# Strassen chains with two additions, a third PSUM bank seeded from the first, and x's first two tiles loaded and turned ahead of the others

## The chip, the cores and the metric

The kernel runs on one core of a Trainium2 chip. The metric is the device time of one execution in microseconds. Before the change it is 2528.57 us, the median of three runs (2528.29 to 2528.87).

In the profile's names PE is TensorE, DVE VectorE, ACT ScalarE, POOL GpSimd and SP SyncE. PEld is TensorE's weight load.

## The reference

Two graph-attention layers over a dense adjacency matrix, a residual and a layernorm, then one binary graph convolution with a residual and a layernorm. N is 3327 rows of 512.

```python
def _gat_layer(x, W, adj):
    proj = x @ W
    Wh, Ws = jnp.split(proj, 2, axis=-1)
    scores = Wh @ Ws.T
    a = jax.nn.softmax(scores, axis=-1) * adj
    out = a @ Wh
    out = out + x
    return jax.nn.leaky_relu(out, NEG_SLOPE)
...
x = _layernorm(x + gat(gat(x)))
bw = jnp.sign(weight)
ba = jnp.maximum(jnp.sign(x), 0.0)
x = _layernorm(x + relu(adj @ (ba @ bw.T)))
```

## The kernel before

Rows are cut into 26 tiles of 128. Two tiles are a pair or half (13 of them, `NQ`), four tiles a column chunk c (7 of them, `NC`; chunks 0 to 5 hold two halves, chunk 6 one). Everything on TensorE is f32, and one f32 product of 128x128 by 128x256 shows as two matmuls.

Each of the two layers has two stages. **Projection** (`project`, 0 to 185 us and 1229 to 1387 us): x's tiles are loaded and turned, the values `wh` are computed per pair, and the queries `g` per chunk. Both use Strassen's scheme with seven products (`seven`, L180): left sums S1 to S4, right sums T1 to T4, seven products over three PSUM banks Z, X and Y, and additions that join them into c11, c12, c21 and c22. The operands for the next stage are stored in HBM: keys per pair (`xs_d`: A11, A12, A21, A22, S1 to S4), values (`ws_d`) and queries per chunk (`gs_d`: B11, B21, B22, T1 to T4). Lists of steps are interleaved by `weave`. Layer 0 starts with x's first four tiles (`transpose_first`), whose turns, the first chain, and the turns of the weights (`transpose_w`, tile pwT, copied out to wTs) alternate.

**Attention** (`attention`, the rest): for every chunk c and pair q one score chain of seven products of two k-halves, spread over two steps (s = 0 and 1), and for every (g, q) one values step. Scores run `LOOK` = 30 steps ahead of the values, so the first 30 steps of a layer hold scores alone. A step's work is a list of (position, action), sorted by position; that is the program order of every engine. In a score chain: z1, x2, add11, z6 and y5 in the first step, z7, add22, y3, add12 and z4 in the second. A product's result that another addition needs is copied out of PSUM by ScalarE (p1, u2, p5, u3); add11 and add22 are VectorE additions, add11 and add12 with one PSUM operand, add22 (L648) with two SBUF operands. c21 is a ScalarE copy of Z.

After a half's last pair its column maximum is taken (`column_max`): fold and turn (L699, L702), a reduction (L703), four tiny copies that bring 32-row parts together (L709), a reduction (L710), three tiny copies (L714), and a transpose that spreads the result into the SBUF tile `off` (L719). A values step then subtracts `off` from a score tile (`shift`, L763), takes the exponential on ScalarE, multiplies with the adjacency, adds the running total, and feeds seven products (L839). When a half is finished its total is turned on TensorE in a PSUM tile of its own (`norm` in `finish`, L890).

SP issues all loads in program order, POOL's queue nearly all stores. Key tiles `xs` are loaded per chain in two parts (512 and 384 KB), each with two buffers, and the query tile `gs` (seven parts of 256 KB for a whole chunk, two buffers) in seven loads spread over the chunk before. `ws` has three buffers, `adj` four.

The finale multiplies the binary parts, and ends with the last three row tiles: a linear part (pxw), moments, root and `scaled`, which stores.

Before any of this, 20 small matmuls (`beat`) run on TensorE.

Of the kernel before, what the change touches and what calls it, by code (L numbers as in the profile page):

```python
# [9 lines left out]
F32 = mybir.dt.float32  # L10
# [19 lines left out]
DRUM = 20  # L30
# [3 lines left out]
def kernel(  # L34
# [44 lines left out]
    SBUFS = LOOK + 3  # L79
# [5 lines left out]
    with tc.manual_schedule():  # L85
        make_identity(nc, ident)
        drum = keep.tile([P, P], BF16, name="drum")
        nc.vector.memset(drum, 0.0)
        beat = ps_tr.tile([P, P], F32, tag="tr", name="beat")
        for n in range(DRUM):  # L90
            nc.tensor.matmul(beat, drum, drum, start=True, stop=True)
# [23 lines left out]
    xs_d = [tc.dram_tile([NQ, P, 8, 2, P], F32, name=f"xs_d{l}") for l in range(L)]  # L115
    ws_d = [tc.dram_tile([NQ, P, 4, HD], F32, name=f"ws_d{l}") for l in range(L)]
    gs_d = [
        [tc.dram_tile([P, 7, 2, len(halves_of(c)) * P], F32, name=f"gs_d{l}_{c}")
         for c in range(NC)] for l in range(L)
# [57 lines left out]
    S1, S2, A11, A12, A21, A22, S3, S4 = range(8)  # L177
    B11, B21, B22, T4, T1, T2, T3 = range(7)

    def seven(lane, name, multiply, c11, c12, c21, c22):  # L180
# [10 lines left out]
        def copied(i, b):  # L191
            if not held:
                two = slot([P, 2, HW], F32, f"h0_{name}"), slot([P, 2, HW], F32, f"h1_{name}")
                held.update(zip(("p1", "p5", "u2", "u3"), (t[:, e] for t in two for e in (0, 1))))
            nc.scalar.copy(held[i], bank[b])

        def add(to, a, b):
            nc.vector.tensor_tensor(to, a, b, ALU.add)

        return [  # L200
            lambda: (product(1, "Z", True), copied("p1", "Z")),
            lambda: (product(2, "X", True), add(c11, bank["X"], held["p1"])),
            lambda: (product(6, "Z", False), copied("u2", "Z")),
            lambda: (product(5, "Y", True), copied("p5", "Y")),
            lambda: (product(7, "Z", False), copied("u3", "Z"),
                     add(c22, held["p5"], held["u3"])),
            lambda: (product(3, "Y", False), add(c12, bank["Y"], held["u2"])),
            lambda: (product(4, "Z", False), nc.scalar.copy(c21, bank["Z"])),
# [27 lines left out]

    ch_lane, acc_lane, tr_lane = (ps_ch, "ch"), (ps_acc, "acc"), (ps_tr, "tr")
# [9 lines left out]
    def key_sums(l, q, a, xT, between=lambda: None):  # L247
# [6 lines left out]
            A22: xT[:, 2:4, j2], S1: s12[:, 0], S2: s12[:, 1], S3: s34[:, 0],  # L254
            S4: s34[:, 1], "s12": s12, "s34": s34,
# [4 lines left out]
        return of  # L260

# [37 lines left out]
    def sums_w(l):  # L299


        wsum_of[l] = ops.tile([P, 4, 2, HD], F32, tag="gs", name=f"wsum_{l}")
# [28 lines left out]
    def project(l, pre):  # L331
# [4 lines left out]
        def load_x(c):  # L336
            rows_of[c] = []
            for t in tiles_of(c):
# [11 lines left out]
        def transpose_first(lane):  # L350

            pool, tag = lane
            xTs[0] = pre.tile([P, KD, CW], F32, tag="xT", bufs=2, name=f"xT_{l}_0")
            pts = [pool.tile([P, CW], F32, tag=tag, name=f"pxt_{l}_{k}") for k in range(KD)]
            xts = [t.rearrange("r (p k) -> r k p", k=KD) for t in rows_of[0]]

            for a in range(CT):
                for k in range(KD):
                    nc.tensor.transpose(pts[k][:, ts(a, P)], xts[a][:, k], ident)
                if a % 2:  # L360
                    for k in range(KD):
                        half = ts(a // 2, HW)
                        copy_out(k, xTs[0][:, k, half], pts[k][:, half])
# [7 lines left out]
        if l == 0:  # L371
            load_x(0)
        else:
            xTs[0] = x_first[l]
        wa = pre.tile([P, KD, D], F32, tag="wa", bufs=1, name=f"wa_{l}")
        for k in range(KD):
            nc.sync.dma_start(out=wa[:, k], in_=w_rows_of(l, 0, k))
        if l == 0:
            load_w(l, 1)
            for k in range(KD):  # L380
                w_rows[l, 0, k] = wa[:, k]
        load_x(1)
        if l == 0:
            transpose_first(acc_lane)
# [17 lines left out]
        def keys(c, a, between=lambda: None):  # L402

            q = c * CT // 2 + a
            of = keys_first.pop((l, q), None) or key_sums(l, q, a, xTs[c], between)
            to = xs_d[l][q]
            for raw in (A11, A12, A21, A22):
                nc.gpsimd.dma_start(out=to[:, raw], in_=of[raw])
            nc.gpsimd.dma_start(out=to[:, S1 : S2 + 1], in_=of["s12"])
            nc.gpsimd.dma_start(out=to[:, S3 : S4 + 1], in_=of["s34"])  # L410
            return of

        def project_values(c, a, lane, between=lambda: None):
# [18 lines left out]

            return (
# [4 lines left out]
        def queries(c, lanes):  # L438
# [15 lines left out]
            if len(halves_of(c)) == 1:  # L454
# [14 lines left out]
                return None, [lambda e=e: one(e) for e in range(KD)] + [last_sums], []  # L469
# [29 lines left out]
            return sums, one, two + [done]  # L499
# [11 lines left out]
        chains, pairs_of, rest = {}, {}, []  # L511
# [6 lines left out]
        if l == 0:  # L518
# [6 lines left out]
            turns = [lambda k=k: transpose_w(l, 0, k, tr_lane) for k in range(KD)]  # L525
            turns += [second.pop(0), lambda: None]
            turns += [lambda k=k: transpose_w(l, 1, k, tr_lane) for k in range(KD)]
            for do in first + second[:2]:
                do()
                turns.pop(0)()  # L530
            second = second[2:]
# [10 lines left out]
        for c in range(NC):  # L542
            turns = []
            if c + 1 < NC:
# [3 lines left out]
                pairs_of[c + 1] = project_values(c + 1, 0, acc_lane)  # L548
                turns += [pairs_of[c + 1].pop(0), lambda: prepare(c + 1)]
            turns = rest + turns  # L550
            rest = [chains[c][1].pop()] if chains[c][1] else []
# [4 lines left out]
            else:  # L556
                one, two = chains[c]
                pairs = pairs_of[c]
                for a in range(1, len(tiles_of(c)) // 2):
                    pairs += project_values(c, a, acc_lane)  # L560
                rest.append(pairs.pop())
                weave(one + two, pairs, turns)
# [12 lines left out]
    def attention(l, att):  # L575
# [8 lines left out]

        def load_gs(c, i, n=1):
            if i == 0:
                gs[c] = ops.tile(
                    [P, 7, 2, len(halves_of(c)) * P], F32, tag="gs", bufs=2, name=f"gs_{l}_{c}"
                )
            nc.sync.dma_start(out=gs[c][:, i : i + n], in_=gs_d[l][c][:, i : i + n])  # L590

        def load_xs(c, q):
            for i, (a, n) in enumerate(((S1, 4), (A22, 3))):
                t = ops.tile([P, 4 - i, 2, P], F32, tag=f"xs{i}", name=f"xs{i}_{l}_{c}_{q}")
                nc.sync.dma_start(out=t[:, :n], in_=xs_d[l][q][:, a : a + n])
                for e in range(n):
                    xs[c, q, a + e] = t[:, e]

        def product(c, q, bank, a, b, start):
# [4 lines left out]
            for k in range(2):  # L604
                nc.tensor.matmul(  # L605
                    ch[bank], xs[c, q, a][:, k], gs[c][:, b, k],
                    start=(start and k == 0), stop=(k == 1), skip_group_check=True,
                )

        def scores(c, q, s):  # L610


# [12 lines left out]
            def z1():  # L625
                product(c, q, "Z", A11, B11, True)
                copied("p1", "Z")

            def x2():
                product(c, q, "X", A12, B21, True)  # L630

            def add11():
                nc.vector.tensor_tensor(c11, ch["X"], ch["p1"], ALU.add)

            def z6():
                product(c, q, "Z", S2, T2, False)
                copied("u2", "Z")
# [5 lines left out]
            def z7():  # L643
                product(c, q, "Z", S3, T3, False)
                copied("u3", "Z")

            def add22():
                nc.vector.tensor_tensor(c22, ch["p5"], ch["u3"], ALU.add)  # L648
# [6 lines left out]

            def z4():
# [3 lines left out]
            def maximum(i):  # L660
                t = sc[i, q]
                if q == NQ - 1 and pad:
                    nc.vector.tensor_scalar(
                        t[:, 1], t[:, 1], there[:, 0:1], there[:, 1:2], ALU.mult, ALU.add
                    )
                if q == 1:
# [742 lines left out]
```

## Time and profile before

| what | us |
|---|---|
| median of three runs | 2528.57 |
| the profiled execution, time | 2527.47 |
| its span | 2525.7 |
| TensorE busy | 2506.7 |
| VectorE busy | 2026.5 |
| POOL busy | 1463.2 |
| ScalarE busy | 783.6 |
| DMA, mean | 249 GB/s, 628.83 MB |

The span covers the work on the engines; the time of an execution has 1.8 us around it. A row of a group reads: line, engine, operation, output<-input, shape, number, then busy us in total, mean ns of one, and the idle time before it with what ended it. The granted TensorE clock was 0.999 of full over the span. Times of timeline rows are from the span's start.

### The profile page before, as it was taken

Reading aid. Unit: us, or ns where it says so; the run is one execution under the profiler, and the core shown is the slowest. Engines: PE = TensorE matmul, PEld = TensorE weight load, DVE = VectorE, ACT = ScalarE, POOL = GpSimd, SP = SyncE. Lnnn points to the kernel's source line nnn. Section 1 sums busy time; section 2 is a strip of 40 time slices with the busy share of each in tenths; the row PEclk is TensorE's granted clock in tenths of the full one; section 3 lists DMA queues with packets and bytes.
Section 4 is the critical chain, followed back from the end, with each engine's and each line's share of the span. In section 5 each row is a group of like instructions: output and inputs, shape, how many; then the busy total and the mean of one; then the engine's idle time right before and its main releaser. Section 6 shows DMA issues by size and latency. Waiting matters only on the chain.

```text
span 2525.7 us, 39290 instructions
## 1 busy us (share of the span) xinstructions
PE 2506.7 (99%) x12257; PEld 2185.0 (87%) x12257; DVE 2026.5 (80%) x3755; ACT 783.6 (31%) x1823; POOL 1463.2 (58%) x2302
## 2 busy tenths in 40 slices
PE   9999999999999999999999999999999999999998
PEld 7888888888888888898888888888888888899876
DVE  5765878789787897869876587888888888898977
ACT  3323333333333233222232333332333323322234
POOL 2652566766666666556655256566666666655631
PEclk9999999999999999999999999999999999999999
DMA  6858777777767767797885877777777777778984
GB/s 207 295 199 236 231 248 231 248 251 238 247 232 250 250 230 241 251 320 264 261 290 206 252 238 241 249 251 259 238 255 244 248 258 236 245 261 302 311 283 165
DMA packets 311394, 628.83 MB, mean 249 GB/s; under 512 B 35819, under 2 KB 166755, under 8 KB 310924
## 3 DMA queue, kind: packets, MB, share of 16 engines
q1 hardware_dynamic: 278254, 529.13, 64.3%
q0 software_dynamic: 32896, 97.09, 10.4%
q8 instruction: 100, 1.64, 0.3%
q14 instruction: 114, 0.93, 0.1%
q10 hardware_dynamic: 30, 0.03, 0.0%
HBM read 528.54 MB, written 97.58 MB: 248 GB/s over the span
## 4 chain that ended last, share of the span: by engine, by line
PE 94%; DVE 4%; issue 1%; POOL 1%; DMA 0%; ACT 0%; SPq 0%; ACTq 0%; DVEq 0%; POOLq 0%
PE acc L839 37%; PE pZ L605 22%; PE pY L605 11%; PE pX L605 6%; PE pZ_wh L421 4%; PE pZ_g L483 3%; PE agg L1137 3%; PE pY_wh L421 2%; PE pY_g L483 2%; PE pm L323 1%; PE pxw L1230 1%; PE pX_wh L421 1%; PE pX_g L483 1%; DVE s L763 1%; PE pg L458 1%
## 5 line engine op out<-in xcount | busy, mean ns | idle before, releaser
L605 PE MATMUL pZ<-gs,xs 128*128 128x256 f32 (+1 forms) x2912 | 699.1, 364 | 0.5 <-ACT u L623 0.4
L605 PEld LDWEIGHTS pZ<-gs,xs 128*128 128x128 f32 x2912 | 536.5, 190 | 71.7 <-ACT p L623 0.9
L812 POOL TENSOR_TENSOR as<-s 128x128 f32<-128x128 f32 x338 | 167.9, 497 | 592.5 <-DVE s L779 412.3
L839 PE MATMUL acc<-ws,s 128*128 128x256 f32 x1352 | 402.2, 379 | 0.0
L605 PE MATMUL pY<-gs,xs 128*128 128x256 f32 (+1 forms) x1456 | 352.1, 364 | 1.1 <-ACT p L623 1.1
L839 PE MATMUL acc<-ws,as 128*128 128x256 f32 x1352 | 349.5, 380 | 2.0 <-POOL as L814 2.0
L839 PE MATMUL acc<-wh,s 128*128 128x256 f32 x1352 | 349.0, 379 | 0.0
L792 POOL TENSOR_TENSOR deg<-deg,adj 128x256 fp8e4<-128x256 fp8e4 x338 | 278.8, 825 | 51.8 <-DMA adj<-in_adjT_dram 37.5
L671 DVE TENSOR_TENSOR top<-top,s 128x512 f32<-128x512 f32 x286 | 249.5, 878 | 69.8 <-ACT s L658 67.0
L605 PEld LDWEIGHTS pY<-gs,xs 128*128 128x128 f32 x1456 | 268.2, 190 | 36.8 <-ACT p L623 1.8
L763 DVE TENSOR_TENSOR s<-s,off 128x512 f32<-128x512 f32 x338 | 297.1, 879 | 0.6
L839 PEld LDWEIGHTS acc<-ws,as 128*128 128x128 f32 x1352 | 251.2, 190 | 40.5 <-POOL as L814 4.8
L839 PEld LDWEIGHTS acc<-ws,s 128*128 128x128 f32 x1352 | 252.9, 190 | 32.2
L839 PEld LDWEIGHTS acc<-wh,s 128*128 128x128 f32 x1352 | 251.6, 190 | 33.5 <-DVE s L779 0.3
L769 ACT ACTIVATE s<-s 128x512 f32<-128x512 f32 x338 | 213.4, 631 | 196.1 <-DVE s L763 193.9
L774 DVE TENSOR_TENSOR total<-total,s 128x512 f32<-128x512 f32 x312 | 270.0, 865 | 0.0
L623 ACT COPY u<-pZ 128x256 f32<-128x256 f32 (+1 forms) x364 | 129.8, 357 | 422.6 <-PE pZ L605 417.5
L648 DVE TENSOR_TENSOR s<-p,u 128x256 f32<-128x256 f32 (+1 forms) x182 | 86.6, 476 | 216.7 <-ACT u L623 216.0
L779 DVE TENSOR_TENSOR s<-s,adj 128x512 f32<-128x512 f32 x338 | 245.9, 728 | 5.0
L813 POOL TENSOR_TENSOR s<-s 128x128 f32<-128x128 f32 x338 | 233.3, 690 | 26.9
L814 POOL TENSOR_TENSOR as<-s 128x128 f32<-128x128 f32 x338 | 225.7, 668 | 26.5
L815 POOL TENSOR_TENSOR as<-s,as 128x128 f32<-128x128 f32 x338 | 206.1, 610 | 26.5
(198 smaller groups left out, 3457.2 us busy)
## 6 DMA issues: line engine op xcount, KB each, us to landing
ws<-ws_d SPq DMA_DIRECT2D x338, 512.0 KB
xs<-xs_d SPq DMA_DIRECT2D x182, 512.0 KB
adj<-in_adjT_dram SPq DMA_DIRECT2D x351, 256.0 KB
xs<-xs_d SPq DMA_DIRECT2D x182, 384.0 KB
gs_d<-gsp POOLq DMA_DIRECT2D x84, 256.0 KB, 2.9
gs<-gs_d SPq DMA_DIRECT2D x70, 256.0 KB
xs_d<-xT POOLq DMA_DIRECT2D x104, 128.0 KB, 3.3
xs_d<-s POOLq DMA_DIRECT2D x52, 256.0 KB, 3.1
```

The lines of the kernel that those rows point to most:

```text
L421: nc.tensor.matmul(bank, of[LEFT[i]][:, k], wr[RIGHT[i]][:, k], start=(start and k == 0), stop=(k == 1), skip_group_check=True,)
L605: nc.tensor.matmul(ch[bank], xs[c, q, a][:, k], gs[c][:, b, k], start=(start and k == 0), stop=(k == 1), skip_group_check=True,)
L671: nc.vector.tensor_tensor(top[i], top[i], t, ALU.max)
L763: nc.vector.tensor_tensor(s, s, off[g].to_broadcast([P, 2, HW]), ALU.subtract)
L769: nc.scalar.activation(sc[g, q], sc[g, q], AF.Exp)
L774: nc.vector.tensor_tensor(total[g], total[g], sc[g, q], ALU.add)
L779: nc.vector.tensor_tensor(s, s, adj[g, q], ALU.mult)
L792: nc.gpsimd.tensor_tensor(deg[:, g], deg[:, g], adj[g, q][:, a], ALU.add, saturate=False)
L813: nc.gpsimd.tensor_tensor(a21, a21, a22, ALU.add)
L814: nc.gpsimd.tensor_tensor(s2, a21, a11, ALU.subtract)
L815: nc.gpsimd.tensor_tensor(s4, a12, s2, ALU.subtract)
L839: nc.tensor.matmul(acc[g][i // 2][:, i % 2], a[i], b[i], start=(q == 0 and i % 2 == 0), stop=(q == NQ - 1), skip_group_check=True,)
```

## The change

The order of the seven products is now 1, 5, 6, 3, 7, 2, 4. Bank X is filled by a ScalarE copy of Z after product 1, and product 2 is accumulated onto it, so c11 is a ScalarE copy of X in place of a copy of p1 and an addition. c22 is added straight out of bank Z. Two VectorE additions per chain are left, and five ScalarE copies as before. `seven` and the score chains change alike.

```diff
-            lambda: (product(1, "Z", True), copied("p1", "Z")),
-            lambda: (product(2, "X", True), add(c11, bank["X"], held["p1"])),
+            lambda: (product(1, "Z", True), seeded()),
+            lambda: (product(5, "Y", True), copied("p5", "Y")),
             lambda: (product(6, "Z", False), copied("u2", "Z")),
-            lambda: (product(5, "Y", True), copied("p5", "Y")),
-            lambda: (product(7, "Z", False), copied("u3", "Z"),
-                     add(c22, held["p5"], held["u3"])),
             lambda: (product(3, "Y", False), add(c12, bank["Y"], held["u2"])),
+            lambda: (product(7, "Z", False), add(c22, bank["Z"], held["p5"])),
+            lambda: (product(2, "X", False), nc.scalar.copy(c11, bank["X"])),
             lambda: (product(4, "Z", False), nc.scalar.copy(c21, bank["Z"])),
...
+        def seeded():
+            bank["X"] = pool.tile([P, HW], F32, tag=tag, name=f"pX_{name}")
+            nc.scalar.copy(bank["X"], bank["Z"])
...
-                return [(0.06, z1), (0.31, x2), (0.45, add11), (0.56, z6), (0.81, y5)]
+                return [(0.06, z1), (0.31, y5), (0.56, z6), (0.81, y3), (0.94, add12)]
             return [
-                (0.02, z7), (0.2, add22), (0.35, y3), (0.5, add12), (0.68, z4),
-            ] + [(0.62, lambda i=i: maximum(i)) for i in mine[1:]]
+                (0.02, z7), (0.15, add22), (0.35, x2), (0.68, z4),
+            ] + [(0.62, lambda i=i: maximum(i, q)) for i in mine[1:]]
```

At the start x's tiles 0 and 1 are loaded and turned first, then wa is loaded, then tiles 2 and 3, which are turned after the first chain's third product. The beats are 15 of 256 columns over seven banks, and three more begin layer 1.

```diff
         if l == 0:
-            load_x(0)
+            load_x(0, slice(0, 2))
         else:
             xTs[0] = x_first[l]
+            for n in range(3):
+                beat(ch_lane, 1)
         wa = pre.tile([P, KD, D], F32, tag="wa", bufs=1, name=f"wa_{l}")
         for k in range(KD):
             nc.sync.dma_start(out=wa[:, k], in_=w_rows_of(l, 0, k))
         if l == 0:
+            load_x(0, slice(2, 4))
             load_w(l, 1)
...
             turns = [lambda k=k: transpose_w(l, 0, k, tr_lane) for k in range(KD)]
+            turns.insert(2, lambda: transpose_first(acc_lane, 1))
             turns += [second.pop(0), lambda: None]
             turns += [lambda k=k: transpose_w(l, 1, k, tr_lane) for k in range(KD)]
-            for do in first + second[:2]:
+            for do in first + second[:3]:
```

The diff also brings a scheme for four pairs' worth of products at once (`quad_sums`, `quad_scores`), for the groups named in `QUADS`. That is `((), ())`, so none of it is run. What belongs to it and is run for every chunk: ten differences of query parts (`query_sums`, two of the chunk's columns in five tiles), 70 stores of them to `ge_d`, and 70 loads of them into the query buffer not in use, in steps 1 to 5 of a chunk. No product reads them.

```diff
+B11, T1, T2, B22, T3, B21, T4 = range(7)
+QUADS = ((), ())
...
+        def first():
+            sub(23, gs[B11][:, 0], gs[T3][:, 1])
+            sub(22, gs[B21][:, 1], gs[T4][:, 0])
+            sub(2, gs[T3][:, 1], b12[:, 0])
+            sub(5, at[22], gs[B22][:, 1])
+            sub(3, at[22], gs[T3][:, 0])
+            store(0, 4)
...
+            more_of[c] = [done] + query_sums(l, c, gs, b12)
```

The query tile becomes two single buffers, `ga` of seven parts and `gb` of five. Parts 0 to 4 alternate between them by chunk; parts 5 and 6 (B21, read by x2, and T4, read by z4) always lie in `ga`. Parts 0 to 4 of the next chunk are loaded in steps 20 to 24, parts 5 and 6 in step 0 of their own chunk. The key tile is one buffer of 896 KB (two of them), loaded in two parts; raw A21 is no longer stored.

```diff
+        ga = ops.tile([P, 7, 2, HW], F32, tag="ga", bufs=1, name=f"ga_{l}")
+        gb = ops.tile([P, 5, 2, HW], F32, tag="gb", bufs=1, name=f"gb_{l}")
...
-            c, i = divmod(u - 7, 2 * NQ)
-            if 0 <= c < NC - 1 and i % 2 == 0 and i // 2 < 7:
-                load_gs(c + 1, i // 2)
+            c, i = divmod(u, 2 * NQ)
+            if 0 <= c < NC - 1 and 20 <= i < 25:
+                load_gs(c + 1, i - 20)
+            if 0 < c < NC and i == 0:
+                load_gs(c, 5, 2)
+            if 0 <= c < NC and 1 <= i < 6:
+                load_ge(c, i - 1)
```

In `column_max` the seven tiny copies go from VectorE to ScalarE. The maximum is copied by ScalarE into a PSUM bank (`beside`), from which `shift` reads it; the other half of this bank takes the turned totals of `norm`. The running total stands later in the step.

```diff
-                    nc.vector.tensor_copy(quad[:B, a], part[ts(a, B)])
+                    nc.scalar.copy(quad[:B, a], part[ts(a, B)])
...
-                    nc.vector.tensor_copy(whole[ts(a, B)], whole[:B])
+                    nc.scalar.copy(whole[ts(a, B)], whole[:B])
...
+        def spread(g):
+            nc.scalar.copy(beside[l][:, 0], off[g])
+
         def shift(g, q):
             s = sc[g, q]
-            nc.vector.tensor_tensor(s, s, off[g].to_broadcast([P, 2, HW]), ALU.subtract)
+            at = beside[l][:, 0:1]
+            nc.vector.tensor_tensor(s, s, at.to_broadcast([P, 2, HW]), ALU.subtract)
...
-            pz = ps_tr.tile([P, 2, P], F32, tag="tr", name=f"pz_{l}_{g}")
+            pz = beside[l][:, 1].rearrange("p (i r) -> p i r", i=2)
...
-                work += [(0.01, lambda: running(*s2)), (0.4, lambda: masked(*s2))]
+                work += [(0.2, lambda: running(*s2)), (0.4, lambda: masked(*s2))]
```

Smaller edits: score slots 33 to 35, one slot for a chain's kept results in place of two, `adj_b` with three buffers in place of two, the packed binary tiles in score slots, one linear part's place in the finale, and the last 15 rows of the output stored by POOL's queue in place of ScalarE's.

```diff
-    SBUFS = LOOK + 3
+    SBUFS = LOOK + 5
...
-        at = {NT - 4: NQ - 0.52, NT - 3: NQ - 0.38}.get(t, at)
+        at = {NT - 6: NQ - 1.46, NT - 4: NQ - 0.52, NT - 3: NQ - 0.38}.get(t, at)
...
-            moments(t1, pw[t1], lambda: scaled(t2, nc.sync, nc.scalar, by_act=True))
+            moments(t1, pw[t1], lambda: scaled(t2, nc.sync, nc.gpsimd, by_act=True))
```

## The prediction

> **What bounds the kernel now.** I read the busy line and the chain first, then busy time by stage, then the few places where TensorE stands idle.
>
> ```profile
> PE 2506.7 (99%) x12257; PEld 2185.0 (87%) x12257; DVE 2026.5 (80%) x3755; ACT 783.6 (31%) x1823; POOL 1463.2 (58%) x2302
> ...
> PE 94%; DVE 4%; issue 1%; POOL 1%; DMA 0%; ACT 0%; SPq 0%; ACTq 0%; DVEq 0%; POOLq 0%
> ```
>
> ```profile
> core 0: us, PE busy (x) PEld busy (x) DVE busy (x) ACT busy (x) POOL busy (x), PEclk, DMA share, GB/s
> 0.00:185.00 185.00, 182.62 (x830) 153.67 (x831) 126.91 (x272) 55.53 (x141) 87.20 (x151) 1.00 0.67 233
> ...
> 275.00:1229.00 954.00, 952.04 (x4565) 835.29 (x4564) 779.46 (x1385) 286.08 (x659) 612.39 (x958) 1.00 0.76 249
> 1229.00:1387.00 158.00, 158.00 (x735) 139.09 (x734) 121.58 (x249) 48.38 (x128) 94.87 (x153) 1.00 0.72 253
> ```
>
> TensorE bounds every stage: all its idle time is 2525.7 − 2506.7 = 19.0 us. The change leaves the number of products alone (7 per chain before and after; the lists of groups that would save products, QUADS, are empty). So a gain can only come out of these 19 us, of which 10.2 lie behind the last matmul (2515.5 to 2525.7). A loss is any new wait. The other gaps, by the timeline: some 3 us in the first 20; 271 to 324 (3.1 together, mostly behind VectorE) and its like at 1473 to 1481 (1.2); 1174 to 1184, 2293, and 2373 to 2414 (3.8 together, VectorE late); 2500 (0.9).
>
> ```profile
> 5.88 2.31 PE L359 MATMUL pxt<-ident,xr 128*128 128x128 f32 x8 [0.25 <-DVE xT L159]
> 7.99 1.91 PE L421 MATMUL pZ_wh<-wa,xT 128*128 128x256 f32 x4
> ...
> 17.19 0.60 PE L272 MATMUL pwT<-ident,w 128*128 128x128 f32 x4
> 18.47 0.66 PE L272 MATMUL pwT<-ident,w 128*128 128x128 f32 x4 [0.68 <-ACT wTs L274]
> ...
> 271.64 1.13 PE L605 MATMUL pX<-gs,xs 128*128 128x256 f32 x4 [0.42 <-DVE s L654]
> ```
>
> And three steps of the chain that ended last (start, length):
>
> ```profile
> 267.11 0.46 DVE top L702
> ...
> 268.34 0.07 DVE mx L709
> ...
> 2518.72 0.63 ACTq L129
> ```
>
> In turn: the first product waits until x's fourth tile is turned; two neighbouring turns of weights stand behind one ScalarE copy; the first column maximum (fold, turn, tiny copies) holds VectorE, and the next chunk's chain comes late; ScalarE issues a DMA inside the tail chain.
>
> **The change, part by part.** The profiled execution took 2527.47 us, 1.8 more than its span; the median is 2528.57. I add the terms to the median.
>
> *Start.* After the change tiles 0 and 1 are loaded first, then the four pieces of wa, then tiles 2 and 3. Eight turns run, then the first product. Its second half needs the fourth DMA, which before landed for TensorE at 7.07, so it ends near 7.9, not 9.90. The next turns need the sixth DMA, some 8.6 by spacing of 0.75 to 0.9 a DMA; they end near 9.1 against 10.76. But eight turns now come later: 8 × 0.11 = 0.9 at full rate. That leaves −0.7 if nothing waits. The copy wait at 18.47 goes, since a product now stands between the two turns (−0.68). Against it, early matmuls run at half pace: the same four matmuls take 0.43 us apart at 8 us and 0.21 after 10.8; if full pace comes at the same moment, work put earlier is done at double price and the −0.7 is nothing. Value −1.0; bounds −2.6 (landings a DMA earlier) and +0.7 (the second product waits for its weight sums, four adds of 0.42, behind the sixth DMA).
> The Trainium skill, "TensorE: Matmul & The Clock Gate", "What's actually happening", says that the clock is gated to half until activity has filled a window of about 3.4 us, and falls back after an idle one. The half pace up to 10.8 agrees. By that rule, gaps that the new DMA order makes between 5.6 and 8 could put full pace one window later: half of 3.4, an estimated 1.7 us more, and the start would be +0.7.
>
> *Chains.* Per chain one add of two SBUF tiles goes (add11), the second add reads PSUM, and ScalarE makes five copies as before.
>
> ```profile
> L763 DVE TENSOR_TENSOR s<-s,off 128x512 f32<-128x512 f32 x338 | 297.1, 879 | 0.6
> ...
> L648 DVE TENSOR_TENSOR s<-p,u 128x256 f32<-128x256 f32 x156 | 78.0, 500 | 203.0 <-ACT u L623 202.2 <-POOL as L815 0.8
> L654 DVE TENSOR_TENSOR s<-pY,u 128x256 f32<-128x256 f32 x156 | 65.4, 419 | 9.4 <-PE pY L605 9.1
> ```
>
> VectorE is freed of 182 × 0.42 (add11) = 76 us, 182 × 0.08 (500 to 419) = 15, 182 tiny copies of 0.25 to 0.29 = 48, and in 338 shifts, which now take the maximum from PSUM, 338 × 0.19 (879 to 0.69, L1239's 512 columns out of PSUM) = 64. None of it is on the path, except in the late gaps: of 3.8 us I take 1.5 (bounds 0 and 3.8), since running sums also stand later in the step. The new wait, z4 for add22, has room: in the present order z4 starts a median 1.50 us after add22's end, and the new add starts one ScalarE copy (0.37) sooner. Where that room was missing (−3.0 to −1.7, the first two chains of chunk 1 in each layer) is the next part. Behind a late z4 stands all of TensorE.
> One bank is now read by the shift and written by the turns at a group's end, so those turns wait for the shift ahead of them. In the trace each of the 26 begins at least 0.84 us after that shift's end: nothing.
> "PSUM — Partial Sum Buffer", "PSUM bank collisions raise a hardware error", of the skill goes further: any two engines in one bank and quadrant must be kept apart. If each of the 26 had to sit out a shift of 0.88 it would be 23 us; the row says 0.
>
> *Chunk 1.* The tiny copies move to ScalarE, seven of 0.25 or so with a VectorE step between, in front of the copy of u2 that z7 waits for. VectorE's fold, turn and reduce end at 268.0, ScalarE's copies some 1 to 2 us later, so z7 (slot 267.60) and all behind it wait about 2.7 us. It replaces 3.1 us of gaps in layer 0 and 1.2 in layer 1: 5.4 − 4.3 = +1.1, and with query operands landing some 0.4 late, +1.5. Bounds: −4.3 (copies finish in time) and +5.4 (old gaps stay).
>
> *Query operands.* Held in two buffers before, in one now. Parts 0 to 4 of a chunk come during the chunk before; parts 5 and 6 can be fetched only after its last z4, behind ws (512 KB), adj (256) and a whole key tile (896) on SP's queue. Adding up that queue's packets in the trace, the key tile lands 7.4 to 7.8 after that z4. 256 KB more is 0.7 to 1.0, so part 5 is there at 8.2 to 8.8. x2, its first reader, has its slot at +8.90 in chunks 2 to 5, +6.82 in chunk 6, where 128 KB land near 8.1. So 0.2 each for eight boundaries, +1.8 with a semaphore's delay, bounds 0 and 4; and 1.35 twice, +2.7, bounds 0.5 and 4. Everything on TensorE stands behind x2.
>
> *Projection.* Ten subtractions per chunk (query_sums, 0.34 each by the pitch, 3.5 us) make extra sums that no product reads. VectorE was busy 126.9 of 185 and 121.6 of 158; the second gets 5 to 6 × 3.5 − adds saved. The sums S1 end 0.43 to 0.91 before the slot that y5 now has; the subtractions use up VectorE's 2.3 idle us per chunk and push S1 some 1 us. And layer 1's first chains wait near 1.0 for the x sums. +3.5, bounds 0 (hidden) and +8 (0.6 in all 14 chunks).
>
> *Transfers.* 70 stores (0.55 us of POOL's issue each, 26 of A21 less) and 70 loads, 16.6 MB each way less 3.4: +4.7% on 628.8 MB. They go in steps 1 to 5 of a chunk at a DMA share of 0.76 and are waited for by nobody; without that cover, 256 KB is 0.7 us per load. I take 0; +5 is the upper bound, in chunk 6 and chunk 1, where it adds to the above.
>
> *Beats, tail.* Fifteen beats instead of 20; three begin layer 1: 3 × 0.11 = +0.3. In the tail ScalarE's issue of 0.63 goes to POOL (−0.6), and an earlier row puts 2500's 0.9 gap partly away (−0.5); bounds −1.5 and 0.
>
> Sum: −1.0 −1.5 +1.5 +1.8 +2.7 +3.5 +0.3 −1.1 = +6.2, so 2534.8, say 2535.
>
> **Rivals.**
> *No change, about 2529.* Query_sums hides in VectorE's idle time and part 5 arrives in time in chunks 2 to 5: without 3.5 and 1.8 the sum is +0.9. For it: VectorE is at 69% in the first projection. Against: S1's margin is under a microsecond, and one VectorE runs in order. In this case the change does little of what it says: the new sums are dead work, the saved adds are off the path.
> *Faster, about 2519.* VectorE's lead of some 200 us over two layers removes every gap that it made: 4.3 in chunk 1, 3.8 late, with start −1.0 and tail −1.1: −10.2. It decides if the tiny copies on ScalarE are done before z7 is due and part 5 lands before x2. For it: most gaps name VectorE. Against: the slots at +6.82, and ScalarE is in order too.
> *Much slower, about 2550.* SP's queue stands at the chunk boundary behind the single-buffered parts, and the loads of ws and adj behind them come late as well: 12 boundaries × 1.3 more (two loads' 0.7 each) is +15. Against: ws is held three deep.
>
> **Numbers.** Forecast 0.43, no change 0.33, faster 0.18, much slower 0.06. A change within 0.2% (5 us, 2523.5 to 2533.6) can't be told from none; so faster 0.18, same 0.33, slower 0.49. The range takes in no change and part of the faster case: 2522 to 2546; the forecast's own is 2530 to 2542.
>
> **What would show it.** Idle of pX behind the DMA of query parts at chunk 6 (some 1.3 us) and near none in 2 to 5; pZ behind ScalarE's u2 copy after 267; pY behind VectorE's sums in 20 to 185 and 1229 to 1387; the first product near 6 to 7 us; no ScalarE issue in the tail; VectorE's busy time some 150 us lower (203 and the chains' 50 adds in the projection less 140 subtractions). Wrong, if TensorE's idle time stays under 19 us, or if a matmul group's pitch is changed.

## The result, and the profile after

The changed kernel takes 2544.61 us (median of six, 2539.39 to 2545.85) against 2528.72 (six, 2527.9 to 2531.38): ratio 1.0056, 95% interval 1.0043 to 1.0069. It is slower, as forecast, by more than forecast. Its profiled execution is the longest of the six, 2545.85 us; its span is 2544.0, 18.3 more than before.

The busy line and the chain of the changed kernel, from the page:

```profile
PE 2511.1 (99%) x12252; PEld 2184.6 (86%) x12252; DVE 1805.5 (71%) x3481; ACT 826.6 (32%) x2031; POOL 1405.2 (55%) x2347
...
PE 93%; DMA 3%; DVE 2%; SPq 1%; issue 0%; ACT 0%; POOL 0%; DVEq 0%; POOLq 0%; ACTq 0%
```

VectorE has 221 us less to do, and it helps little. TensorE's idle time went from 19.0 to 32.9 us, and its busy time grew by 4.4 us for the same products. DMA now holds 3% of the chain, where it held 0%. The waits of TensorE (what it waited for, us in total, times, longest) name the transfer:

```profile
PE pX L771 <- DMA ga<-gs_d: 11.1, 10, 2.7
PE pZ L771 <- ACT u L885: 3.9, 4, 1.7
PE pZ L771 <- DVE s L910: 2.6, 3, 1.0
PE pY L771 <- ACT p L885: 1.5, 2, 0.7
```

`ga<-gs_d` on pX is part 5 of the queries, the operand of x2. Where the time went is read best by setting the start of the same matmuls in both traces side by side:

| TensorE reaches | before | after | shift |
|---|---|---|---|
| first query product, layer 0 (the weight products are done) | 39.68 | 37.12 | −2.56 |
| chunk 1, layer 0 | 264.14 | 264.08 | −0.07 |
| chunk 2 | 412.53 | 412.15 | −0.38 |
| chunk 6 | 1042.80 | 1044.77 | +1.96 |
| layer 0's last score product | 1161.47 | 1166.35 | +4.87 |
| layer 1's first product | 1228.99 | 1233.20 | +4.20 |
| chunk 1, layer 1 | 1465.55 | 1473.10 | +7.55 |
| chunk 2 | 1612.04 | 1620.76 | +8.72 |
| chunk 6 | 2242.31 | 2259.05 | +16.74 |
| layer 1's last score product | 2361.79 | 2382.82 | +21.03 |
| the last matmul | 2515.15 | 2533.27 | +18.12 |
| end of the span | 2525.7 | 2544.0 | +18.3 |

The steps between the rows give a ledger: start −2.6; first chains of both attentions and layer 1's projection +5.8 (2.49 and 3.35); chunk 1 of both layers +0.9; chunks 2 to 6, from each chunk 2's start to the last score product, +17.6 (5.25 and 12.31); the ends of the layers −3.6 (−0.67 and −2.91); the tail +0.2.

Of the 17.6 us, 11.1 are the ten waits above. A wait costs more than its idle time, which is counted from the modelled end of the matmul before: chunk 2 of layer 0 loses 0.62 us with a wait of 0.35, and the six other chunks that have a wait of x2 and nothing else differ from it in the same way, by 0.26 to 0.27. Ten times this is 2.7. Some 3 are a slower clock, which comes next. The last 0.5 is a wait of z for ScalarE's u2 in chunk 6 of layer 0.

The largest item, in the timeline of the changed kernel (start, length, idle before it):

```profile
1786.66 1.03 PE L1092 MATMUL acc<-wh,s 128*128 128x256 f32 x4
1790.42 2.04 PE L771 MATMUL pX<-ga,xs 128*128 128x256 f32 x4 [2.74 <-DMA ga<-gs_d]
1792.25 1.85 PE L1092 MATMUL acc<-ws,as 128*128 128x256 f32 x4
1793.94 0.59 PE L1092 MATMUL acc<-ws,s 128*128 128x256 f32 x2
1794.37 1.03 PE L771 MATMUL pZ<-ga,xs 128*128 128x256 f32 x4
```

and TensorE's granted clock around it, from the windows (PEclk is the third number from the end):

```profile
core 0: us, PE busy (x) PEld busy (x) DVE busy (x) ACT busy (x) POOL busy (x), PEclk, DMA share, GB/s
1788.00:1794.00 6.00, 3.58 (x9) 2.88 (x10) 3.08 (x6) 0.38 (x2) 2.90 (x5) 0.72 0.50 186
```

x2 stands idle for 2.74 us, and then four matmuls take 2.04 us where the same group takes 1.03 a moment later: eight are 0.43 us apart instead of 0.21. The clock of 0.72 in this window says the same. It happens again behind the 2.42 us wait of chunk 6 (2268), and not behind the 2.11 us one at 1053. So the transfer costs its wait and, where that is long, some 1.3 to 1.7 us more; this is most of TensorE's added busy time. It may be part of why the six executions spread over 6 us; only one of them was profiled.

### The profile page after: what moved, and what is told of

Its sections match the earlier page's. It is cut to its first block, busy times and chain, and to the rows that moved or that the text cites. A ratio compares the mean times of both kernels' runs of the same rounds, so it can differ in the third digit from the quotient of the medians.

```text
span 2544.0 us, 38721 instructions
## 1 busy us (share of the span) xinstructions
PE 2511.1 (99%) x12252; PEld 2184.6 (86%) x12252; DVE 1805.5 (71%) x3481; ACT 826.6 (32%) x2031; POOL 1405.2 (55%) x2347
## 3 DMA queue, kind: packets, MB, share of 16 engines
q0 software_dynamic: 36960, 110.76, 11.8%
## 4 chain that ended last, share of the span: by engine, by line
PE 93%; DMA 3%; DVE 2%; SPq 1%; issue 0%; ACT 0%; POOL 0%; DVEq 0%; POOLq 0%; ACTq 0%
PE acc L1092 38%; PE pZ L771 22%; PE pY L771 11%; PE pX L771 6%; PE pZ_wh L558 3%; PE pZ_g L622 3%; PE agg L1404 3%; DMA ga<-gs_d 3%; PE pY_wh L558 2%; PE pY_g L622 2%; PE pm L455 1%; PE pxw L1497 1%; PE pX_g L622 1%; PE pX_wh L558 1%; PE pg L596 1%
## 5 line engine op out<-in xcount | busy, mean ns | idle before, releaser
L1065 POOL TENSOR_TENSOR as<-s 128x128 f32<-128x128 f32 x338 | 218.9, 648 | 678.8 <-DVE s L1032 595.7
L771 PE MATMUL pZ<-ga,xs 128*128 128x256 f32 (+1 forms) x1976 | 460.2, 357 | 3.2 <-DVE s L910 2.6
L771 PEld LDWEIGHTS pZ<-ga,xs 128*128 128x128 f32 x1976 | 358.4, 190 | 51.5 <-DVE s L910 4.3
L904 DVE TENSOR_TENSOR s<-pY,u 128x256 f32<-128x256 f32 (+1 forms) x182 | 73.5, 404 | 315.2 <-PE pY L771 278.2
L771 PE MATMUL pZ<-gb,xs 128*128 128x256 f32 x936 | 240.4, 379 | 3.4 <-ACT u L885 3.4
L1016 DVE TENSOR_TENSOR s<-s,beside 128x512 f32<-128x512 f32 x338 | 228.7, 677 | 1.1 <-ACT beside L1011 0.9
L1027 DVE TENSOR_TENSOR total<-total,s 128x512 f32<-128x512 f32 x312 | 221.7, 711 | 0.0
L771 PEld LDWEIGHTS pZ<-gb,xs 128*128 128x128 f32 x936 | 177.7, 190 | 28.3 <-ACT u L885 4.2
L1092 PE MATMUL acc<-wh,as 128*128 128x256 f32 x676 | 201.2, 379 | 0.0
L771 PE MATMUL pY<-ga,xs 128*128 128x256 f32 (+1 forms) x832 | 192.0, 353 | 1.5 <-ACT p L885 1.5
```

Source lines behind the costliest of these rows:

```text
L771: nc.tensor.matmul(ch[bank], xs[c, q, a][:, k], query(c, b)[:, k], start=(start and k == 0), stop=(k == 1), skip_group_check=True,)
L1016: nc.vector.tensor_tensor(s, s, at.to_broadcast([P, 2, HW]), ALU.subtract)
L1027: nc.vector.tensor_tensor(total[g], total[g], sc[g, q], ALU.add)
L1065: nc.gpsimd.tensor_tensor(s3, a11, a21, ALU.subtract)
L1092: nc.tensor.matmul(acc[g][i // 2][:, i % 2], a[i], b[i], start=(q == 0 and i % 2 == 0), stop=(q == NQ - 1), skip_group_check=True,)
```

## The experiments

Each is compared with runs of the kernel before on the same chip (median 2528.1 to 2528.5; 2529.8 for the last one).

**Parts 5 and 6 asked for first.** The loads of the query parts go to the head of step 0.

```diff
             u = v + LOOK
+            c, i = divmod(u, 2 * NQ)
+            if 0 < c < NC and i == 0:
+                load_gs(c, 5, 2)
...
-            if 0 < c < NC and i == 0:
-                load_gs(c, 5, 2)
```

> The changed kernel, but query parts 5 and 6 are asked for at the head of a chunk's step 0, ahead of ws, adj and the key tile. Theory Q (the place in SP's queue behind a single buffer is the loss): x2's waits for part 5 in chunks 2 to 6 of both layers (15 to 17.5 us with the slow clock after two of them) go, time 2526 to 2531. Rival T (the 4.7% more traffic makes such loads late wherever they stand): at least half of the waits stay, time 2536 or more.

2530.94 us, ratio 1.0009 (0.9999 to 1.0019). In TensorE's waits pX is gone, one of 0.5 us for a key tile is new, and the three others are as they were:

```profile
PE pZ L771 <- ACT u L885: 3.9, 4, 1.7
PE pZ L771 <- DVE s L910: 2.6, 3, 1.0
PE pY L771 <- ACT p L885: 1.5, 2, 0.7
```

From chunk 2 to chunk 6 the shift against the kernel before stays at +1.94 in layer 0 and +6.38 in layer 1, to a hundredth: these stretches lose nothing. The same bytes are moved by the same queue. Theory Q holds, the traffic is not the cause.

**A second whole buffer.**

```diff
-        gb = ops.tile([P, 5, 2, HW], F32, tag="gb", bufs=1, name=f"gb_{l}")
+        gb = ops.tile([P, 7, 2, HW], F32, tag="gb", bufs=1, name=f"gb_{l}")
...
-            if c % 2 and i < 5:
+            if c % 2:
...
-            if 0 <= c < NC - 1 and 20 <= i < 25:
-                load_gs(c + 1, i - 20)
-            if 0 < c < NC and i == 0:
-                load_gs(c, 5, 2)
+            if 0 <= c < NC - 1 and 19 <= i < 26:
+                load_gs(c + 1, i - 19)
...
-    SBUFS = LOOK + 5
+    SBUFS = LOOK + 3
```

> The changed kernel, but the second query buffer has seven parts too, so all seven come in steps 19 to 25 of the chunk before; two score slots less to make room. Theory Q: no wait of x2 on a query part at all, time 2525 to 2530, like the run with the early place or a little less. Rival T: the waits move to key or value tiles and the time stays above 2536.

2530.41 us, 1.0006 (0.9997 to 1.0016): the same as the early place, within 1 us, and a trifle above what was expected of it. Either cure gives back 14 us.

**Without the extra sums.** The ten differences per chunk, their stores and loads are left out.

```diff
-            more_of[c] = [done] + query_sums(l, c, gs, b12)
+            more_of[c] = [done]
...
-            if 0 <= c < NC and 1 <= i < 6:
-                load_ge(c, i - 1)
```

> The changed kernel without the ten differences of query parts, their 70 stores and 70 loads (no product reads them). Theory Q: the x2 waits stay, since those loads stand behind parts 5 and 6 in the queue; only the first chains of each layer's attention gain (2.5 us of waits per layer, mostly gone), time 2538 to 2542. Rival T: part 5 lands sooner, most x2 waits go, time below 2532.

2539.01 us, 1.0045 (1.0029 to 1.0062). From the end of the weight products to chunk 1 layer 0 now loses 0.0 us instead of 2.49, layer 1's stretch 0.7 instead of 3.35. By the medians 5.6 us are won, near the 5.1 of these two stretches. x2's waits stay, if smaller in this execution (6.5 us in 9; the longest, 1.8, is followed by no half pace):

```profile
PE pX L770 <- DMA ga<-gs_d: 6.5, 9, 1.8
PE pZ L770 <- ACT u L884: 3.9, 4, 1.7
```

How those sums cost time shows in the changed kernel's chain at layer 0's first score chain:

```profile
187.49 0.56 DVE ge L370 x3
...
188.76 0.43 DVE t L251
...
190.19 0.34 DVE s L910
190.53 0.04 issue
190.57 1.56 PE pZ L771 x6
```

Sums of chunk 6's queries that nobody reads (ge) stand on VectorE ahead of the value sums (t) and of the addition out of bank Z (L910), for which z4 waits 1.01 us. Another 0.74 goes at y3, whose p5 copy ScalarE reaches late. In the projection itself no wait for them is seen: layer 0 has none, and layer 1's one of 0.58 us (1244, for VectorE's wh) is there without them too, with 0.27.

**The start alone**, put into the kernel before (loads and turns of x's first tiles as in the diff, nothing else).

> The kernel before with the new start alone: x's tiles 0 and 1 loaded and turned first, tiles 2 and 3 behind wa and turned after the first chain's third product. Theory: the 2.6 us by which the weight products end earlier are a gain of their own, time 2525.5 to 2527. Rival: they are given back at the first chains of the attention, time 2528 to 2529.

2527.11 us, 0.9996 (0.9986 to 1.0005): −1.1 by the medians, between the two ranges, and this comparison can't tell it from nothing. In its profile the weight products end 2.36 us earlier and chunk 6 of layer 0 still begins 2.27 earlier: the first chains give nothing back. Some 1.0 us is lost later, in chunk 6 of that layer, where z waits for a key tile's load (0.45 and 0.10 us). How much of the 2.36 is the new order's is told below.

**Both cures together** (whole second buffer, no extra sums).

> Both cures in one: seven parts in the second query buffer, and no differences of query parts with their stores and loads. Theory: the two add up, since they act in different places (chunk boundaries, first chains of the attention): 2530.4 less 2 x 2.5, time 2524.5 to 2527. Rival: the first chains' waits only move on to the next VectorE wait, time 2528 or more.

2526.21 us, 0.9989 (0.9980 to 0.9999). They add up: 2530.4 less the two stretches' 5.1 is 2525.3, and this is 0.9 above it.

**The tiny copies later in the step**, on top of that.

```diff
-            return [(-0.04, fold), (0.2, turn), (0.5, across), (0.7, back)]
+            return [(-0.04, fold), (0.2, turn), (0.6, across), (0.7, back)]
```

What it aims at, in the changed kernel's chain at chunk 1: seven tiny copies on ScalarE, 0.2 us each with a VectorE reduction between, and only then the copy of u2 that z7 needs.

```profile
267.87 0.20 ACT mx L956
268.08 0.02 issue
268.10 0.21 DVE mx L957
...
268.75 0.19 ACT mx L961
268.94 0.02 issue
268.96 0.38 ACT u L885
269.34 0.04 issue
269.39 1.13 PE pZ L771 x4
```

> The run before this one in the list, but the tiny copies of a chunk's first column maximum stand at 0.60 of the step instead of 0.50, so ScalarE copies u2 for z7 ahead of them. Theory: z7's wait for u2 in chunk 1 (1.7 us by the trace, twice) goes and some of the 0.6 behind it, 3 to 4 us in all. Rival: the maximum comes later, and shift and the products behind it wait as long: no change (within 1 us).

2524.64 us, 0.9985 (0.9975 to 0.9995): 1.6 us, half of what the theory said. z7's wait is gone, and two products later z4 waits for VectorE:

```profile
269.33 1.99 PE L770 MATMUL pZ<-gb,xs 128*128 128x256 f32 x8 [1.52 <-DVE s L909]
```

In chunk 1 only 0.2 us per layer was won. The rest came in chunk 6, which this run passes 1.2 us (layer 0) and 0.5 us (layer 1) sooner than the run before it.

**Parts 5 and 6 later still.** In the changed kernel, `i == 0` becomes `i == 1`.

> The changed kernel with parts 5 and 6 asked for one step later still: the suspected cost enlarged. In chunks 2 to 5 a step is 6.04 us, so each of these eight waits of x2 grows by 4 to 6 us, those of chunk 6 by 3 to 4. If an idle time over some 2.4 us is what puts TensorE to half pace, every such wait is now followed by matmuls 0.43 us apart for 1 to 4 us, and the time is 2600 to 2630; if the two slow stretches in the changed kernel's profile came by chance, few of them are, and the time is 2590 to 2605.

2596.16 us (one execution). The waits grew less than expected (to 3.4 to 5.3 us), so the time lies in the rival's range, and the time alone settles nothing. The trace does. Two of the ten waits:

```profile
425.38 2.08 PE L771 MATMUL pX<-ga,xs 128*128 128x256 f32 x4 [3.42 <-DMA ga<-gs_d]
427.25 1.91 PE L1092 MATMUL acc<-ws,as 128*128 128x256 f32 x4
...
432.22 1.03 PE L771 MATMUL pZ<-ga,xs 128*128 128x256 f32 x4
```

```profile
1992.68 1.13 PE L771 MATMUL pX<-ga,xs 128*128 128x256 f32 x4 [3.46 <-DMA ga<-gs_d]
1993.65 1.03 PE L1092 MATMUL acc<-ws,as 128*128 128x256 f32 x4
```

Behind nine of the ten, matmuls 0.43 us apart are found until 3.6 to 5.7 us after the wait's end, as at 425. Behind the one at 1992, as long as the first, they don't. So the half pace follows long waits, but not each of them. What decides stands in the traces' own record of the granted clock. In all 14 profiles it changes only at the edges of equal steps of 3.41 us: full or half for one or more whole steps (in the changed kernel half from 1790.50 to 1793.91 and from 2268.36 to 2271.78). The steps around the two waits (two of the first, three of the second):

```profile
core 0: us, PE busy (x) PEld busy (x) DVE busy (x) ACT busy (x) POOL busy (x), PEclk, DMA share, GB/s
420.95:424.36 3.41, 1.01 (x5) 0.56 (x3) 3.16 (x8) 1.26 (x2) 1.45 (x3) 1.00 0.93 304
424.36:427.77 3.41, 2.38 (x6) 1.94 (x7) 3.27 (x6) 0.22 (x1) 2.51 (x5) 0.50 0.49 179
...
1987.67:1991.08 3.41, 1.55 (x8) 1.02 (x6) 3.17 (x6) 1.26 (x2) 1.92 (x4) 1.00 0.83 264
1991.08:1994.49 3.41, 1.81 (x8) 1.63 (x9) 1.94 (x4) 0.37 (x1) 2.54 (x5) 1.00 0.62 226
1994.49:1997.90 3.41, 3.41 (x17) 3.00 (x16) 0.00 (x0) 0.48 (x2) 1.25 (x3) 1.00 0.12 19
```

Of the first wait 2.40 us fall into one step, and the next step has half the clock. An edge cuts the second wait, of 3.46 us, into 1.85 and 1.60, and the clock stays. Counted over all profiles, without their first and last 20 us, 11 full-pace steps hold 2.11 us of idle time or more, and each is followed by a step at half pace; more than 10,000 hold 1.95 or less, and none is. The 2.11 us wait at 1053 is such a case: an edge at 1053.22 leaves 1.84 of idle time in one step. So the length of a wait and its place on this raster decide together.

**The chains alone**, put into the kernel before with the beats that belong to them (order of products, seeded bank, two additions, in projection and attention).

> The kernel before with the new chains alone (order of products, seeded bank, two additions), and the beats over all banks that go with the seeds. Theory: the chain by itself costs TensorE nothing and gives VectorE some 90 us, which takes a part of the waits behind VectorE late in each layer: 2524 to 2528. Rival: z4's new wait for the addition out of its own bank shows at chunk 1 and in the projection, time 2530 or more.

2530.88 us, 1.0009 (1.0000 to 1.0019), 2.7 us above the kernel before of the same call. The rival's time and, in chunk 1, its wait are there (not in the projection). The chain by itself is no gain; that it is a loss stands at the edge of what the comparison can tell:

```profile
PE pZ L618 <- DVE s L661: 4.0, 4, 1.5
PE acc L850 <- POOL as L825: 2.1, 4, 0.8
PE pZ L618 <- DMA xs<-xs_d: 1.1, 1, 1.1
```

L661 is the addition out of bank Z, for which z4 now waits in chunk 1 of both layers, twice in each: 4.0 us, where the kernel before has waits of 2.2 in these chunks. The 1.1 us at 1099, in chunk 6, are for a key tile's load and need not come from the chain: the start alone and both cures have 0.4 to 0.5 there. The waits behind POOL, late in the layers, are what they were, though VectorE has an addition less per chain. The kernel before:

```profile
PE acc L839 <- POOL as L814: 2.0, 4, 0.8
```

**The end's last store**, on top of the later tiny copies: the last 15 rows of the output by ScalarE's queue again, or by SP's.

```diff
-            moments(t1, pw[t1], lambda: scaled(t2, nc.sync, nc.gpsimd, by_act=True))
+            moments(t1, pw[t1], lambda: scaled(t2, nc.sync, nc.scalar, by_act=True))
```

> The last run (two buffers, no extra sums, tiny copies at 0.60) with the last 15 rows of the output stored by ScalarE's queue again. Theory: in all runs with POOL's queue the program ends with POOL's drain, which lasts 5.6 to 8.0 us behind that store; without it the drain is over early, ScalarE's issue costs 0.63 again, and the end comes 5.2 us behind the last scaling as in the kernel before: 2524.6 - 2.9 + 0.6, time 2521.5 to 2523. Rival: the end waits for the store's landing whichever queue sends it: 2524 to 2525.5.

2521.89 us, 0.9976 (0.9966 to 0.9986).

> The same with those 15 rows stored by SP's queue, which stands idle there: no issue of ScalarE's ahead of the root and no store for POOL to drain. Theory: 0.6 us less than with ScalarE's queue, 2521 to 2522.5. Rival (SP's two issues in a row delay the last tile's store): no better than ScalarE's queue.

2522.80 us, 0.9977 (0.9968 to 0.9986): not better than ScalarE's queue, as the rival said. From the last matmul's end to the end of the program it takes 11.2 us, with ScalarE's queue 9.9: SP's last issue comes 0.6 us sooner, but lasts 1.93 us in place of 0.33. In the changed kernel POOL issues that store at 2537.10:

```profile
2537.10 0.52 POOL L154 DMA_DIRECT2D out_dram<-ho  x1 [4.13 <-ACT ho L1531]
```

In the trace's instructions a drain of POOL follows, from 2537.51 to 2543.14, and the program ends 0.84 us behind it. In the run before these two the drain lasts from 2514.29 to 2522.26, with the end at 2523.09. With ScalarE's queue it begins at 2508.85, is over at 2516.69, and the end, at 2519.81, waits for other things. So the saved 0.63 us of ScalarE's issue was paid back by POOL's drain.

**The maximum read from SBUF again**, on the same base, with POOL's queue at the end.

```diff
-            at = beside[l][:, 0:1]
+            at = off[g].rearrange("p (a w) -> p a w", a=1)
```

> The run before these two (two buffers, no extra sums, tiny copies at 0.60, POOL's queue at the end) with the maximum read by shift from SBUF again, not from PSUM. Theory: a shift takes 0.88 us again in place of 0.68, VectorE gets 60 us more, and the waits behind VectorE late in each layer come back (3.8 us in the kernel before): 2526.5 to 2529. Rival: the waits there went by the other relief of VectorE (one addition less per chain), and shift is worth nothing: 2524 to 2525.5.

2527.51 us, 0.9996 (0.9987 to 1.0005), 2.9 more than with PSUM (2.6, if each is set against the kernel before of its own call). VectorE's rows say why; first this run, then the changed kernel (677 in this run's base too):

```profile
L1015 DVE TENSOR_TENSOR s<-s,off 128x512 f32<-128x512 f32 x338 | 290.4, 859 | 0.0
```

```profile
L1016 DVE TENSOR_TENSOR s<-s,beside 128x512 f32<-128x512 f32 x338 | 228.7, 677 | 1.1 <-ACT beside L1011 0.9
```

182 ns a shift, 62 us in all. The running total, which nothing was done to, goes from 714 ns to 797 as well, and VectorE is busy 84.1 us more than in the base run. The waits at 2292 and 2397 to 2411 are back, the latter behind POOL, whose sums stand behind VectorE's product:

```profile
PE acc L1091 <- POOL as L1066: 1.2, 2, 0.8
```

With PSUM this line is gone; from layer 1's last score product to the last matmul this run loses 2.1 us against the other. So the gain at the layers' ends came from shift's operand. The idle time of shift in the changed kernel is 1.1 us in 338, 0.9 of it for `beside`: the shared bank costs it next to nothing.

**The old score chain in the best version** (own bank for product 2, three additions; u3 shares p1's tile for room).

```diff
-                return [(0.06, z1), (0.31, y5), (0.56, z6), (0.81, y3), (0.94, add12)]
+                return [(0.06, z1), (0.31, x2), (0.45, add11), (0.56, z6), (0.81, y5)]
             return [
-                (0.02, z7), (0.15, add22), (0.35, x2), (0.68, z4),
+                (0.02, z7), (0.2, add22), (0.35, y3), (0.5, add12), (0.68, z4),
```

> The run with ScalarE's queue in the tail (two buffers, no extra sums, tiny copies at 0.60), with the attention's score chains as they were before: own bank for product 2, three VectorE additions, z4 not behind an addition out of its own bank. Theory: the chain alone cost 2.7 us on the kernel before, through z4's waits and through copies of ScalarE that other work waits for; here its waits of chunk 1 (1.5 and 0.6 twice) go, but VectorE is given 76 us more work and the waits late in each layer come back in part: 2520.5 to 2523.5, no clear difference. Rival A (the saved addition is what keeps VectorE in time): 2524 or more. Rival B (the chain is a loss in itself): 2520 or less.

2526.91 us, 0.9989 (0.9980 to 0.9998; the kernel before took 2529.80 in this call). By time this is rival A, by the trace it is not:

```profile
PE pY L770 <- ACT p L885: 6.8, 4, 2.4
PE beat L106 <- DVE drum L100: 1.1, 1, 1.1
```

All four waits lie in chunk 1, where the tiny copies now stand ahead of p5's copy. At the ends of the layers nothing came back, though VectorE is busy 91.7 us more than in the run with ScalarE's queue, and the run before this one added only 84.1. The saved addition is not what keeps VectorE in time there. What the old chain would give with the tiny copies in a place of their own was not tried.

## Why the prediction was right, and where it missed

The direction, and the main mechanism, were right: parts 5 and 6 in a single buffer behind SP's other loads. The time lies near the upper end of the stated range, 2522 to 2546, and above the forecast's own, 2530 to 2542. By terms:

| term | forecast | measured in the profile |
|---|---|---|
| start | −1.0 | −2.6 |
| projection's sums | +3.5 | +5.8, elsewhere |
| chunk 1 | +1.5 | +0.9 |
| query operands, chunks 2 to 6 | +4.5 | +17.6 |
| late gaps, with the one at 2500 | −2.0 | −3.6 |
| beats, tail | −0.3 | +0.2 |

**Query operands: the size failed.** Most of the error is in chunks 2 to 5, where the sign "near none" didn't come: the eight waits there are 6.5 us, of which two in layer 1 (2.74 and 1.57) make up 4.3; chunk 6 has 4.5 in place of 2.7. The step said that part 5 "is there at 8.2 to 8.8", and set that against the slot of x2 at +8.90, which left 0.2 a boundary. Summed up in the same way, its packets do land at 7.9 to 8.6 after the last z4 in the changed kernel. But x2 starts at 9.3 to 9.9 in most chunks, and at 10.6 and 11.8 in two of layer 1: 1.0 to 3.2 us behind the sum. The sum takes the queue's packets as served in order, and they are not: in chunk 3 of layer 1, where it says 8.60, the last of the 128 packets of 3 KB of the key tile, which was asked for ahead of part 5, ends at 9.24. What the rest of the delay is made of stays open. The trace of before had the warning: at the start x's fourth tile landed at 5.65 by the same sum, and TensorE's turn of it began at 7.07. It allowed a "semaphore's delay" and put it inside 1.8 us for eight boundaries, when those two numbers said 1.4 for each. Second, it left out what a wait does to the clock, some 3 of the 17.6 us. (About 0.5 of the 17.6 is not theirs: the run with the early place loses that much in the same stretches.) The rival "much slower" comes nearer by its time, but not by its cause: of ws, adj and the keys behind the query parts, none is waited for.

**Projection: the right cause, in the wrong place.** "push S1 some 1 us" did not happen: TensorE waits for nothing between 20 and 180 us. The extra sums cost time only where VectorE passes from chunk 6's sums to the first score chains, 2.5 us per layer, as the run without them shows.

**Chunk 1** was right in its mechanism: z7 waits behind u2's copy for 1.69 us, in each layer, where 2.7 was said, and part of the old gaps went.

**Late gaps: low, and owed to one relief of four.** VectorE lost 221 us, not 150: besides shift, the running total took 711 ns instead of 865. The prediction counted the saved addition, the second addition, the tiny copies and shift together; the runs show that the waits come back without shift's PSUM operand and not without the saved addition, and that the chain alone gains nothing there and is 2.7 us slower by the medians. The tiny copies were not tried apart. The gaps at 271 to 324 are "mostly behind VectorE" in the prediction; in the trace 1.11 of the 1.82 us of idle time there stand behind ScalarE's copy p (299).

**Tail: wrong sign.** ScalarE's issue left the chain as said, but the store that was moved made POOL's drain the last thing.

**Start: right by the medians (−1.1, which isn't told from nothing), too small by the profile.** The moment at which TensorE comes to full pace is not the same in all executions: the last matmul at half pace ends at 10.98 us in the profile of before, and between 4.0 and 5.6 us in eleven others, whichever start they have. Three are late: before, the early-place run (10.07) and the run with SP's queue (11.14, after a first step at full pace from 4.25 to 7.67). With the new start the gain against the profile of before is 1.7 to 2.7 us with full pace early, and 0.5 and 1.0 with full pace late; the old start with full pace early (the chains alone) gained 0.5. So the new order is worth some 0.5 to 2.2 us, and the rest of the 2.6 is the clock's moment.

The Trainium skill, "TensorE: Matmul & The Clock Gate", "What's actually happening", says that the activity window runs freely and doesn't begin with the kernel, so that the moment varies. These profiles agree: the edges of the 3.41 us steps don't lie at the same distance from the kernel's start in them. It gives an idle window of about 3.4 us for the fall to half pace. Here a step with 2.11 us of idle time was already followed by it, and a wait of 3.46 us that an edge divides was not; the measured times stand.

## What to carry to other kernels

When an operand's buffer is made single, its reload can be asked for only after its last reader; put that request at the head of the queue, and price its arrival by a row where an engine waited for such a load, not by summed bytes. Before an engine that is off the path is relieved, find which of its instructions stands ahead of the wait: here moving one operand from SBUF to PSUM gained 2.6 to 2.9 us and an addition less per chain gained nothing. Where TensorE waits for over 2 us, look at the granted clock behind it. The best version of these runs (second whole buffer, no dead sums, later tiny copies, ScalarE's queue at the end) takes 2521.89 us, 0.24% less than the kernel before.

## What was not expected of the hardware

- TensorE's granted clock changes on a raster of 3.41 us. A full-pace step with 2.11 us of idle time or more was followed by half pace, 11 times of 11, and one with 1.95 or less never, apart from the first and last 20 us of a run (at the start of the run with SP's queue a step with 1.71 was); so 11 of the 12 waits of 2.4 us and more brought it and one, cut by an edge, did not. It lasts one or two steps, so that a wait costs more than its length: eight matmuls at 0.43 us in place of 0.21 are 1.7 us more behind a wait of 2.74, thirteen are 2.8 us more behind one of 3.42.
- A drain of POOL at the end, behind the last store on its queue, took 4.4 us in the kernel before, 5.6 in the changed one, and 4.2 to 8.0 in the others, 7.8 to 8.0 in all seven without the extra sums; why it differs stays open. It matters only where that store is the last thing.
- A load's release came 1.0 to 3.2 us behind the moment at which its queue had moved that many bytes.
